# Transposing fp32 tiles as two 16-bit halves in 64-column tiles, in a fused four-layer graph-attention kernel

## The chip, the cores and the metric

One core of one Trainium2 chip. The metric is the device time of one execution in microseconds (us). All executions quoted here are of the fast state, with a mean granted TensorE clock of 0.995 to 0.997 in every profiled one. Engines: PE is TensorE, DVE is VectorE, ACT is ScalarE, POOL is GpSimd.

## The reference, cut to what matters

Sixteen graphs of 1024 nodes with 256 features, all fp32, one adjacency matrix. Four layers, each of this form:

```python
h = jnp.maximum(_layernorm(x, axis=-1), 0.0)
x = x + layer(h, adj, ...)          # four times

# layers 0 and 3 (four heads of 64 columns) and layer 1 (one head of 256):
q = h @ W
e = leaky_relu(s_src[:, None] + s_dst[None, :], 0.2)   # s = q . a, per node
e = where(adj > 0, e, -big)
out = elu(softmax(e) @ q)
# layer 2: e comes from (h W1)(h W2)^T, and the end is a relu
```

So each layer needs h transposed (features on partitions) for h @ W. These transposes are what the change is mostly about.

## The kernel before

All work is given to a small list scheduler inside the kernel (`plan.add(engine, cost, due, function, waits...)`): it simulates the engines with the costs given and emits the instructions in the resulting order. A cost there is a belief, not a measurement. `wide=True` marks PE work in 128-column shapes, between which and the rest the scheduler tries not to alternate.

Nearly all matrix products run in two column tiles of 64:

```python
def product(to, stationary, moving, start, stop):
    for c in range(0, P, COLS):                 # P = 128, COLS = 64
        nc.tensor.matmul(to[c : c + COLS], stationary[:, c : c + COLS], moving, ...)
```

The transposes of h did not; they are fp32 at the full 128 columns, two or four tiles of h at a time:

```python
run = 2 if direct else 4
...
tp = T["tp", t0] = buf("pp", [P, KC, 2 * P])                       # PSUM, fp32
for k in range(2):
    for c in range(KC):
        nc.tensor.transpose(tp[:, c, k * P : (k + 1) * P], T["h", t0 + k][:, c * P : (c + 1) * P], ident)
...
s = plan.add(PE, 0.44 * n, at, turned, norms, ..., wide=True)
...
nc.scalar.copy(T["hT", t0], T["tp", t0])                           # PSUM to SBUF, 512 words a partition
s = plan.add(ACT, 0.6, at, kept, (s,), ...)
...                                                                # then the projection, `product` with w[:, c, :cols]
cols = F + 3 * heads                                               # 268 columns with four heads, 259 with one
```

After the projection two exponentials per tile are taken of the extra columns and kept as factors; the factors of a layer are transposed too. The vectors `a` of layer 0 come with two transfers of short pieces. In the last layer each half of the nodes is closed (divide, ELU, add, store) for all four heads at once.

## Time and profile before

| of the kernel before | value | from |
|---|---|---|
| time | 3103.51 us (3102.70 to 3105.31, 4 runs) | the runs |
| PE / DVE / ACT busy | 99% / 88% / 44% | the page's first row |
| one steady period (one graph) | 188.3 us | starts of the same copy in neighbouring graphs |
| visits to 128-column shapes | 183 | instruction order |
| PE work, by its records | 2982 us | see below |
| time PE did no work: first 200 us / 200 to 2950 us / rest | 55.2 / 41.2 / 24.9 us | see below |

The last two rows will be used for every kernel. They are worked out, not read: each PE record of the profiled execution (for the kernel before one of 3104.86 us, 1.4 above its median) is counted at its own undisturbed spacing (29.17 ns for 65 columns, 108.75 for 257, 214.8 for 512, and so on, as the prediction lists them; a 16-bit transpose counts 56 ns at 128 columns or without a partner, and 27.9 ns in a pair of 64-column tiles), summed over a stretch, and taken from the stretch's length. A switch of shape counts as lost time in this account, which is good to a few tenths of a us. By the prediction's reading, the 41.2 us left in the middle stretch are the switches and nothing else: 149 of the visits lie there, 0.277 us each. That is why "PE 99% busy" is no reason to stop looking.

### The profile page before, as it was taken

The numbers are of one execution on the slowest core, as the hardware profiler recorded it, in microseconds if no ns is written. First come the engines' busy times: TensorE is split into PE (matmuls) and PEld (weight loads), VectorE is DVE, ScalarE is ACT, GpSimd is POOL, SyncE is SP. The second block draws the span as 40 slices with busy tenths as digits, with TensorE's granted clock in tenths as the row PEclk, the third lists the DMA queues.
The fourth block names the chain that finished last, engine by engine and source line by source line (L and its number), as shares of the span: only waits on it lengthen the run. The fifth ranks groups of instructions, "written<-read, shape, count | busy, mean of one in ns | idle before, by whom it ended". The sixth has DMA issues, their size and how long they took to land.

```text
span 3103.1 us, 108725 instructions
## 1 busy us (share of the span) xinstructions
PE 3058.2 (99%) x48836; PEld 2160.0 (70%) x48836; DVE 2716.4 (88%) x5532; ACT 1354.5 (44%) x3369; POOL 128.3 (4%) x99
## 2 busy tenths in 40 slices
PE   7899999999999999999999999999999999999998
PEld 5776757777676776767767676676767767665766
DVE  7999868999989899898989989899899989787797
ACT  5454465443533445334443433434334453345343
POOL 1000000000000000000000000000000000000000
PEclk9999999999999999999999999999999999999999
DMA  3111002102011110101102011020111101000110
GB/s 127 33 54 33 19 29 73 46 30 60 22 40 46 36 46 23 60 23 36 46 26 60 23 36 47 26 60 22 43 43 33 53 30 39 19 22 29 33 36 24
DMA packets 83577, 123.22 MB, mean 40 GB/s; under 512 B 8544, under 2 KB 44192, under 8 KB 83104
## 3 DMA queue, kind: packets, MB, share of 16 engines
q1 hardware_dynamic: 81776, 115.66, 12.4%
q8 instruction: 385, 6.31, 0.8%
q14 instruction: 88, 0.72, 0.1%
q10 hardware_dynamic: 1328, 0.52, 0.1%
HBM read 98.83 MB, written 17.33 MB: 37 GB/s over the span
## 4 chain that ended last, share of the span: by engine, by line
PE 96%; DVE 2%; DMA 1%; ACT 0%; issue 0%; POOL 0%; SPq 0%; POOLq 0%; DVEq 0%
PE pp L574 32%; PE acc L574 31%; PE accb L574 29%; PE pp L886 4%; DVE p L1063 1%; DMA a_bc<-in_L_gnn_a_dram 1%; DMA raw<-in_adj_dram 0%; DVE bn L800 0%; PE pp L998 0%; DVE xt L1041 0%; PE pp L982 0%; DVE o L1040 0%; DVE mv L801 0%; ACT junk_a L683 0%; POOL rstd L836 0%
## 5 line engine op out<-in xcount | busy, mean ns | idle before, releaser
L1063 DVE SCALAR_TENSOR_TENSOR p<-row,ke,mask 128x512 f32<-128x512 f32 x2048 | 1424.5, 745 | 94.5 <-PE acc L574 91.7
L574 PEld LDWEIGHTS acc<-val,p 128*64 128x64 f32 x32768 | 1066.9, 138 | 202.0 <-issue 109.0
L574 PE MATMUL acc<-val,p 128*64 128x65 f32 x32768 | 1095.4, 223 | 12.1 <-DVE p L1063 11.1
L574 PE MATMUL accb<-val,p 128*64 128x257 f32 x8192 | 926.1, 380 | 0.0
L574 PEld LDWEIGHTS accb<-val,p 128*64 128x64 f32 x8192 | 569.7, 136 | 291.3 <-issue 9.5
L574 PE MATMUL pp<-qT,hT 128*64 128x512 f32 x2048 | 471.5, 593 | 0.0
L574 PE MATMUL pp<-w,hTp 128*64 128x268 f32 (+1 forms) x3072 | 376.3, 388 | 0.7 <-ACT hTp L901 0.7
L1169 ACT ACTIVATE u<-pp 128x512 f32<-128x512 f32 x256 | 152.4, 595 | 323.2 <-PE pp L574 229.4
L574 PEld LDWEIGHTS pp<-w,hTp 128*64 128x64 f32 x3072 | 209.6, 137 | 107.8 <-issue 6.2
L870 ACT ACTIVATE h<-xt,nshift,rstd 128x256 f32<-128x256 f32 x512 | 272.5, 595 | 17.0 <-DVE nshift L839 15.7
L574 PEld LDWEIGHTS pp<-qT,hT 128*64 128x64 f32 x2048 | 133.0, 137 | 190.4 <-issue 184.9
L1209 ACT ACTIVATE o<-accb,rdens 128x256 f32<-128x256 f32 x128 | 60.7, 474 | 424.8 <-DVE rdens L1201 384.9
L800 DVE BATCH_NORM_STATS2 bn<-xt 128x6 f32<-128x256 f32 x512 | 212.5, 415 | 13.6 <-DMA xt<-in_x_dram 4.3
L836 POOL TENSOR_TENSOR rstd<-rstd,neg_half 128x8 f32<-128x8 f32 (+1 forms) x66 | 119.6, 1813 | 2371.9 <-DVE rstd L833 2094.5
L1207 ACT ACTIVATE o<-accb,rden 128x256 f32<-128x256 f32 x128 | 60.7, 475 | 336.4 <-DVE rden L1201 335.5
L1175 DVE TENSOR_TENSOR p<-p,mask 128x512 f32<-128x512 f32 x256 | 177.1, 692 | 8.9
L1142 DVE SCALAR_TENSOR_TENSOR p<-row,ke,mask 128x512 f32<-128x512 f32 x256 | 181.1, 743 | 0.0
L1174 DVE SCALAR_TENSOR_TENSOR p<-u,p 128x512 f32<-128x512 f32 x256 | 174.5, 682 | 5.9 <-ACT p L1170 5.7
L1170 ACT ACTIVATE p<-pp,shift_col 128x512 f32<-128x512 f32 x256 | 174.9, 683 | 0.0
L931 ACT ACTIVATE val<-pp 128x4 f32<-128x4 f32 (+1 forms) x384 | 66.8, 174 | 202.3 <-PE pp L574 202.2
L1040 DVE SCALAR_TENSOR_TENSOR o<-ex,o 128x256 f32<-128x256 f32 (+1 forms) x192 | 131.8, 686 | 16.0 <-ACT ex L1036 16.0
L901 ACT COPY hTp<-pp 128x512 f32<-128x512 f32 x192 | 104.6, 588 | 88.7 <-PE pp L886 88.6
(82 smaller groups left out, 1849.8 us busy)
## 6 DMA issues: line engine op xcount, KB each, us to landing
row<-er_d SPq DMA_DIRECT2D x272, 256.0 KB, 3.2
xt<-in_x_dram SPq DMA_DIRECT2D x32, 512.0 KB, 5.1
out_dram<-xt SPq DMA_DIRECT2D x32, 512.0 KB, 3.1
raw<-in_adj_dram SPq DMA_DIRECT2D x4, 1024.0 KB
raw<-in_adj_dram SPq DMA_DIRECT2D x16, 256.0 KB, 3.2
w<-in_L_gnn_W_dram SPq DMA_DIRECT2D x2, 256.0 KB
a_bc<-in_L_gnn_a_dram SPq DMA_DIRECT2D x4, 128.0 KB, 10.3
wraw<-in_L_gnn_W_dram SPq DMA_DIRECT2D x2, 256.0 KB
```

The source lines that it names most:

```text
L574: nc.tensor.matmul(to[c : c + COLS], stationary[:, c : c + COLS], moving, start=start, stop=stop, skip_group_check=True,)
L800: nc.vector.bn_stats(st, x_tiles[b][:, t, :])
L836: nc.gpsimd.tensor_tensor(T["rstd"][:, its], T["rstd"][:, its], neg_half[:, its], OP.pow)
L870: nc.scalar.activation(h, x_tiles[b][:, t, :], AF.Relu, bias=T["shift"][:, t : t + 1], scale=T["rstd"][:, t : t + 1],)
L886: nc.tensor.transpose(tp[:, c, k * P : (k + 1) * P], T["h", t0 + k][:, c * P : (c + 1) * P], ident)
L1040: nc.vector.scalar_tensor_tensor(o, ex, -1.0, o, op0=OP.mult, op1=OP.max)
L1063: nc.vector.scalar_tensor_tensor(p, lay.rows[half, hd], lay.ke[:, hd, jt : jt + 1], mask_of(half, jt), op0=OP.max, op1=OP.mult)
L1142: nc.vector.scalar_tensor_tensor(p, lay.rows[half, 0], lay.ke[:, 0, jt : jt + 1], mask_of(half, jt), op0=OP.max, op1=OP.mult)
L1169: nc.scalar.activation(u, e, AF.Exp, scale=1.0 - SLOPE)
L1170: nc.scalar.activation(p, e, AF.Exp, bias=shift_col, scale=SLOPE)
L1174: nc.vector.scalar_tensor_tensor(p, u, 1.0, p, op0=OP.max, op1=OP.mult)
L1175: nc.vector.tensor_mul(p, p, mask_of(half, jt))
```

## The change

Its intent: no switches in the steady part. An fp32 tile is read as pairs of 16-bit halves; each half is transposed as 16-bit data, bit for bit, in the two 64-column tiles that the products use; ACT puts the halves together when it copies from PSUM. Around that: one extra column per head less in the projection (one of the two exponentials is taken with a scale instead), vectors `a` in one transfer of 2 KB rows, the exponential's table loaded early, the first four tiles normalised ahead of the next four, and the last half of the last layer closed head by head. The scheduler's start times were fitted anew. The diff's core:

```diff
+    def turn(to, of):
+        n = of.shape[1]
+        for c in range(0, n, COLS):
+            nc.tensor.transpose(to[c : c + COLS], of[:, c : c + COLS], ident_b)
+    def halves(of):
+        return of.bitcast(BF16).rearrange("p (f s) -> p s f", s=2)
...
-                        tp = T["tp", t0] = buf("pp", [P, KC, 2 * P])
+                        tp = T["tp", t0] = buf("pp", [P, 2, KC, 2 * P], BF16)
                         for k in range(2):
+                            bits = halves(T["h", t0 + k])
                             for c in range(KC):
-                                nc.tensor.transpose(... T["h", t0 + k][:, c * P : (c + 1) * P], ident)
+                                for side in range(2):
+                                    turn(tp[:, side, c, k * P : (k + 1) * P], bits[:, side, c * P : (c + 1) * P])
-                s = plan.add(PE, 0.44 * n, at, turned, norms, ..., wide=True)
+                s = plan.add(PE, 0.47 * n, at, turned, norms, ...)
-                    nc.scalar.copy(T["hT", t0], T["tp", t0])
-                s = plan.add(ACT, 0.6, at, kept, (s,), ...)
+                    bits = T["hT", t0].bitcast(U16).rearrange("p c (q s) -> p s c q", s=2)
+                    nc.scalar.copy(bits, T["tp", t0].bitcast(U16))
+                s = plan.add(ACT, 0.95, at, kept, (s,), ...)
...
-            run = 2 if direct else 4
+            run = 2
-            cols = F + 3 * heads if self.gat else F
+            cols = F + 2 * heads if self.gat else F
...                                                 # `a` of a layer in one transfer:
+            queue.dma_start(
+                out=tiles["a"].rearrange("p h s d -> p (h s d)"),
+                in_=bass.AP(tensor=a.tensor, offset=a.offset, ap=[[0, P], [1, own * 2 * d]]),
+            )
...                                                 # front
+    plan.add(ACT, 1.6, SOON, warm)
+                at = due - 2 * (direct and n == 0)
-            stats = [statistics(b, t, due - 1, (loads[b][t],)) for t in range(NT)]
+            stats = [statistics(b, t, due - (3 if t < HT else 1), (loads[b][t],)) for t in range(NT)]
...                                                 # end
+            ending = lay.b == B - 1 and lay.layer == 3 and half == 1
+            if ending:
+                cols, sizes = (hd * d, (hd + 1) * d), (4, 0.8, 0.8)
```

The mask and factor transposes go through `turn` as well (cut here, like the new start times and the sign handling of `a`).

## The prediction

> **What bounds the kernel now.** I read the page first (busy shares, the 40 slices, the chain by line), then the groups by form, then the windows, and then the chain in order of time in one steady period, at the front and at the end.
>
> ```profile
> PE 3058.2 (99%) x48836; PEld 2160.0 (70%) x48836; DVE 2716.4 (88%) x5532; ACT 1354.5 (44%) x3369; POOL 128.3 (4%) x99
> ...
> PE   7899999999999999999999999999999999999998
> ...
> DVE  7999868999989899898989989899899989787797
> ...
> PE pp L574 32%; PE acc L574 31%; PE accb L574 29%; PE pp L886 4%; DVE p L1063 1%; DMA a_bc<-in_L_gnn_a_dram 1%; DMA raw<-in_adj_dram 0%; DVE bn L800 0%; PE pp L998 0%; DVE xt L1041 0%; PE pp L982 0%; DVE o L1040 0%; DVE mv L801 0%; ACT junk_a L683 0%; POOL rstd L836 0%
> ...
> L1063 DVE SCALAR_TENSOR_TENSOR p<-row,ke,mask 128x512 f32<-128x512 f32 x2048 | 1424.5, 745 | 94.5 <-PE acc L574 91.7
> ...
> L901 ACT COPY hTp<-pp 128x512 f32<-128x512 f32 x192 | 104.6, 588 | 88.7 <-PE pp L886 88.6
> ```
>
> The busy row and the slices say that PE works from the second slice to the last but one; the chain by line is 96% PE. DVE is second at 88%, ACT has room. But a busy PE is not a PE that does useful work: one steady stretch of the chain of waits shows what hides in it.
>
> ```profile
> 1025.79 0.47 PE acc L574 x16
> 1026.25 1.02 PE pp L886 x8
> 1027.28 1.08 PE acc L574 x32
> 1028.36 3.48 PE accb L574 x32
> ...
> 1049.29 0.93 PE acc L574 x32
> ```
>
> Thirty-two products take 0.93 us after other products and 1.08 us after eight transposes; and the eight transposes, 109 ns apart in the trace, take 1.02 us and not 0.87. So a visit to the 128-column transposes costs 0.30 us beyond its work. Starts in the trace say where: 152 instead of 52 ns from the last narrow product to the first transpose, 202 instead of 109 ns from the last transpose to the next product, and about 58 ns more between the first transposes. A second way: the chain repeats every 188.3 us (same pieces at 1086.58 and 1274.90). The records of one period at their own spacings (29.17 ns for 65 columns, 108.75 for 257, 214.8 for 512, 113.3 for 268, 109.6 for 259, 108.3 for 256, 109 per transpose) add up to 185.5 us. The missing 2.8 us over 10 visits are 0.277 us each. There is no other stall in the steady part.
>
> Front and end are limited by something else, DVE, since the four-head layers give it 0.66 us per weight tile (spacing in the trace) for 0.47 us of products:
>
> ```profile
> 13.08 0.42 DVE L666 TENSOR_TENSOR wa<-w,a_bc 128x256 f32<-128x256 f32 x1 [2.82 <-DMA a_bc<-in_L_gnn_a_dram]
> ...
> 17.29 1.28 ACT L870 ACT_TABLE_LOAD   x1 [17.29 <-DVE rstd L833]
> ...
> 21.33 5.11 PE L574 MATMUL pp<-w,hTp 128*64 128x268 f32 x32
> ...
> 29.24 2.74 DVE L1063 SCALAR_TENSOR_TENSOR p<-row,ke,mask 128x512 f32<-128x512 f32 x4 [0.30 <-ACT row L986]
> ...
> 38.10 0.76 DVE L940 TENSOR_TENSOR val<-pp,val 128x256 f32<-128x256 f32 x2 [2.67 <-ACT ke L932]
> ```
>
> ```profile
> 3092.53 0.20 DVE rden L1096
> ...
> 3092.75 0.94 ACT o L1107 x4
> ...
> 3093.71 1.06 ACT ex L1035
> ...
> 3094.79 1.06 ACT ex L1036
> ...
> 3095.88 1.24 DVE o L1040
> ...
> 3097.14 1.23 DVE xt L1041
> ```
>
> (The first fence is the timeline at the front, lines left out between; the second the chain at the end.) First weights at 29.24 us after waits for a small-packet load, a table load and the projections; at the end 5.8 us of closing behind the last products, then 4.7 us until the output is stored.
>
> **What the Trainium skill says.** "TensorEngine Tiling (Array Packing)", Key Properties: "Changing tiling mode (not just tile) drains the TensorE". The trace agrees and gives the price, 0.24 to 0.30 us per visit there and back; it is the shape and not the transposing, because a plain 128x128 product (L777) is also followed by 310 ns instead of 216. The same page, Feature Incompatibilities: column tiling excludes transpose mode for fp32 input. Hence the halves[...]. "TensorE: Matmul & The Clock Gate", section "Wait — 56ns, not 53.3ns?": N/2.4 GHz plus 2.5 ns, and starts never closer than about 25 ns. The 16-bit mask transposes here start 56 ns apart, as it says; the floor is not tested before. "ScalarE: Activation LUTs", What ACT_TABLE_LOAD costs: 0.833 ns per element, 1283 ns per load. The copies here (370 ns for 256, 588 for 512) give 0.85 ns, and the one load took 1283.
>
> **The change part by part.** The instruction order of both builds gives counts.
> 1. Visits to 128-column shapes fall from 183 to 18 (the row spreads of the first and last layers, weights, checks). 165 x 0.277 = -45.7 us.
> 2. 1024 fp32 transposes at 109 ns (111.6 us) become 4096 of 64 columns. The two column tiles alternate and should run side by side, as the product records do (starts about 10 ns apart in pairs); so a pair takes the 56 ns of a 16-bit transpose of 128 columns, 28 each, and I take 28.5: 116.7 us, +5.1.
> 3. 268 to 264 columns: 2048 records x 4/2.4 ns = -3.4; 259 to 258: 1024 x 0.42 ns = -0.4. The exponentials from one column less keep their number.
> 4. Factor transposes: 46 x 109 ns against 92 x 56 ns (one tile, no pairs): 0.
> PE work: -44.4 us. All of it at its old work plus switches is 3032.5 us, so 2988 us after.
> 5. ACT: 256 copies of 512 words become 1024 halves each. 588 + 512 x 0.85 ns = 1.02 us, +0.43, in all about +111 us on an engine with over 1700 us idle. Not on the path unless a projection waits for it.
> 6. Front. The vectors `a` come as one 2 KB row per partition, the table is loaded early, the first four tiles are normalised without waiting for the others. I add DVE rows to the second reduction of w0: ready near 17.3 us instead of 20.3. But the new order puts all eight projections ahead of the first row spread, so I expect the first weights near 28 us, not at 25, with 18.3 us of DVE work done instead of 14.5. DVE idle in the front falls by about 5 us there, and about 1 us more from the wait at 38.10. From about 26.4 to 20.5 us.
> 7. Behind it DVE stays the limit: DVE rows up to a weight tile plus all PE work from its products on exceed the PE total by at most 21.9 us before and 24.2 us after. PE gets cheaper, the DVE rows don't.
> 8. End. PE work to the last projection of the last layer, plus the DVE rows left, plus the ACT steps behind the last products: 17.6 us over the PE total before. After: the last quarter closes 256 columns instead of 1024 (2.7 instead of 5.8 us), but the earlier three quarters now stand between the weights on DVE (6 x 0.46 us), and more of the previous layer's weights stand behind that projection: 18.8 us.
> 9. Store: 4.7 to about 4.5.
>
> Before: 3032.5 + 21.9 + 17.6 + 26.4 + 4.7 = 3103.1 (the 26.4 is what was left; the DVE gaps in the trace up to 107 us, about 20, and rows slightly longer than my spacings make it up). After: 2988.2 + 24.2 + 18.8 + 20.5 + 4.5 = 3056 us, 1.5% less.
>
> **Rivals.**
> (a) Issue-bound transposes. Each needs an explicit weight load and a matmul, two instructions in 28 ns. Before, explicit pairs were 56 ns apart, and the products come two records to an instruction; nothing shows 14 ns per instruction. At 40 ns each the change loses 47 us and gains nothing: 3103. At 56 (no pairing) 3168. Against it: the schedule's own cost, 0.47 us for 16, is 29 ns, and its other costs match the trace.
> (b) A new drain between 16-bit and 32-bit products replaces the old one. At 0.1 us each way for some 170 visits, +34 us: 3090. Against it: one fp32 transpose followed by a 16-bit one in the trace took 109 ns, no more.
> (c) DVE becomes the bound in the steady part. It has 169 us of work per period, 90% of 188.3 and 91% of the new 185.6; order was refitted, but single waits may add 5 to 15 us: 3065.
> (d) Front and end gain more than I grant (rearranged on purpose): 10 to 15 us, 3042.
>
> **Range and chances.** The saving in the steady part is well measured, so the middle is narrow: 3045 to 3068 if (a) and (b) are false. I give (a) or (b) in part one chance in five, which stretches the upper side. 3040 to 3084 should hold 8 of 10. Faster by over 2% needs under 3041.5, so it needs (d) nearly whole: 0.15. Slower by 2% needs (a) in full: 0.02. Within 2%: 0.83.
>
> **What would show it.** A steady period near 185.6 us in the chain; 16 transposes in about 0.46 us; products after them at 0.93 us per 32. If the spacing is 40 ns or more, (a); if products after transposes still take longer, (b); gaps before products ended by DVE between 300 and 2800 us, (c). Copies near 1.0 us. First weights near 28 us, closing behind the last products near 2.7 us. The prediction is wrong in its middle if the front's DVE gaps do not shrink or shrink by over 10 us.

## The result, and the profile after

The changed kernel takes 3061.51 us (3061.14 to 3062.39, 4 runs) against 3103.51 us. The ratio is 0.9864, 95% interval 0.9847 to 0.9881: within 2%, a gain of 1.4%. (Ratios are the mean time of one kernel's fast runs over that of the other's fast runs of the same rounds, so not quite the ratio of the medians quoted.) Predicted: 3056, range 3040 to 3084.

From the page of the changed kernel: the busy row, the chain by line, and one group (busy us, mean ns of one, then idle time before):

```profile
PE 3017.0 (99%) x52018; PEld 2467.5 (81%) x52018; DVE 2722.5 (89%) x5551; ACT 1524.6 (50%) x3352; POOL 127.6 (4%) x115
...
PE pp L572 33%; PE accb L572 29%; PE acc L572 29%; PE pp L585 3%; DVE p L1089 3%; ACT hT L918 0%; ACT hTp L918 0%; DVE bn L813 0%; DVE xt L1066 0%; DMA xt<-in_x_dram 0%; DVE o L1065 0%; DVE mv L814 0%; PE pp L1002 0%; PE tpm L585 0%; PE er 
...
L918 ACT COPY hTp<-pp 128x1024 uint16<-128x1024 uint16 x192 | 248.8, 1324 | 54.9 <-PE pp L585 54.8
```

PE still bounds it, and the transposes (now line 585) fell from 4% of the chain to 3%. New in the chain is ACT, with line 918, which is the copy that puts the halves together: 1324 ns each where the old copy took 588 and the prediction said 1020. The chain of waits of the stretch from 1000 to 1120 us shows what it does:

```profile
1069.90 0.47 PE pp L585 x13
1070.37 0.02 issue
1070.40 1.36 ACT hT L918
1071.76 0.04 issue
1071.80 2.81 PE pp L572 x24
...
1079.21 0.89 PE pp L585 x32
1080.10 0.94 PE acc L572 x32
```

The last two lines are the change as intended: 32 transposes in 0.89 us, which is 28 ns each, then 32 products in 0.94 us, the undisturbed value; before, products after transposes took 1.08. These lines show no drain (the time that a switch of shape costs), neither the old one nor a new one between 16-bit and 32-bit data. But the lines above show PE waiting 1.4 us for a copy. In the whole stretch from 200 to 2950 us:

```profile
by line: PE pp L572 34.8%; PE accb L572 30.5%; PE acc L572 29.7%; PE pp L585 3.3%; ACT hT L918 0.5%; ACT hTp L918 0.3%; DVE p L1089 0.3%; issue 0.1%; PE er L585 0.1%; DVE parts L1308 0.1%; DVE bn L813 0.1%; DVE xt L1066 0.1%; DVE o L1065 0.
```

ACT copies hold 0.8% of 2750 us. In the kernel before the same row had no ACT entry:

```profile
by line: PE pp L574 34.2%; PE acc L574 30.7%; PE accb L574 30.4%; PE pp L886 4.3%; PE pp L998 0.3%; PE pp L1273 0.0%
```

The account by stretches:

| | PE work | idle 0 to 200 | idle 200 to 2950 | idle rest | steady period |
|---|---|---|---|---|---|
| before | 2982 us | 55.2 us | 41.2 us | 24.9 us | 188.3 us |
| after | 2981 us | 42.6 us | 10.8 us | 25.6 us | 186.3 us |

So the steady stretch gave 30 us, though the switches alone stood at 41; the front gave 13, PE work 1, and the end took 0.7. The period of 186.3 us misses the 185.6 that the prediction asked for.

At the front the chain in order of time shows the same copy, and the first weights (DVE line 1089):

```profile
25.22 1.32 ACT hTp L918
26.58 2.00 PE pp L572 x16
...
29.42 0.59 ACT row L1006
30.04 4.73 DVE p L1089 x7
```

The first weights come at 30.04 us. Before it was 29.24, and the prediction said 28. At the end, the steps behind the last products:

```profile
3052.60 0.19 DVE rden L1122
...
3054.63 0.42 DVE xt L1066
```

From 3052.60 to 3055.05 is 2.4 us of closing where it was 5.8; the store behind it takes until 3059.6, 4.5 us as predicted.

### The profile page after: what moved, and what is told of

Read it like the earlier page. It is cut to its first block, busy times and chain, and to the rows that moved or that the text cites. A ratio compares the mean times of both kernels' runs of the same rounds, so it can differ in the third digit from the quotient of the medians.

```text
span 3059.6 us, 115063 instructions
## 1 busy us (share of the span) xinstructions
PE 3017.0 (99%) x52018; PEld 2467.5 (81%) x52018; DVE 2722.5 (89%) x5551; ACT 1524.6 (50%) x3352; POOL 127.6 (4%) x115
## 4 chain that ended last, share of the span: by engine, by line
PE 94%; DVE 4%; ACT 1%; issue 0%; DMA 0%; SPq 0%; DVEq 0%; ACTq 0%
PE pp L572 33%; PE accb L572 29%; PE acc L572 29%; PE pp L585 3%; DVE p L1089 3%; ACT hT L918 0%; ACT hTp L918 0%; DVE bn L813 0%; DVE xt L1066 0%; DMA xt<-in_x_dram 0%; DVE o L1065 0%; DVE mv L814 0%; PE pp L1002 0%; PE tpm L585 0%; PE er L585 0%
## 5 line engine op out<-in xcount | busy, mean ns | idle before, releaser
L572 PE MATMUL acc<-val,p 128*64 128x65 f32 x32768 | 1080.9, 223 | 18.2 <-DVE p L1089 17.5
L572 PEld LDWEIGHTS accb<-val,p 128*64 128x64 f32 x8192 | 765.3, 137 | 103.6 <-issue 6.4
L572 PE MATMUL pp<-qT,hT 128*64 128x512 f32 x2048 | 457.7, 592 | 0.0
L572 PE MATMUL pp<-w,hTp 128*64 128x264 f32 (+1 forms) x3072 | 376.9, 386 | 1.3 <-ACT hTp L918 0.3
L572 PEld LDWEIGHTS pp<-qT,hT 128*64 128x64 f32 x2048 | 189.6, 137 | 205.9 <-issue 204.0
L572 PEld LDWEIGHTS pp<-w,hTp 128*64 128x64 f32 x3072 | 241.7, 137 | 81.0 <-ACT hTp L918 8.6
L918 ACT COPY hTp<-pp 128x1024 uint16<-128x1024 uint16 x192 | 248.8, 1324 | 54.9 <-PE pp L585 54.8
L1060 ACT ACTIVATE ex<-o 128x1024 f32<-128x1024 f32 (+1 forms) x195 | 122.1, 626 | 90.2 <-DVE o L1133 85.8
L585 PEld LDWEIGHTS <-h 128*64 128x64 bf16 x4096 | 145.5, 111 | 24.0 <-issue 13.3
```

Source lines behind the costliest of these rows:

```text
L585: nc.tensor.transpose(to[c : c + COLS], of[:, c : c + COLS], ident_b)
L918: nc.scalar.copy(bits, T["tp", t0].bitcast(U16))
L1060: nc.scalar.activation(ex, o, AF.Exp)
```

## The experiments

Two theories of why the steady stretch gave less than its switches. **A**: the halves themselves are fine, and the slow copy, later than the order of instructions assumes, makes PE wait. **B**: something of the halves on PE costs more than it seems (a remaining drain, the issue of twice the instructions), or the switches were worth less than read. Twelve kernels ran; all gave right results; the first one told below computes coarser numbers on purpose and still passed the comparison. The kernel before ran along in each batch; its medians were 3103.12, 3103.38, 3102.91 and 3102.80 us.

### The copy

**Only half of the data.** The changed kernel, but ACT copies the upper halves alone (512 elements, as 16-bit floats widened to fp32):

```diff
-                    bits = T["hT", t0].bitcast(U16).rearrange("p c (q s) -> p s c q", s=2)
-                    nc.scalar.copy(bits, T["tp", t0].bitcast(U16))
+                    nc.scalar.copy(T["hT", t0], T["tp", t0][:, 1])
```

> The changed kernel with ACT copying the upper halves alone, 512 elements instead of 1024 (numbers coarser on purpose, same transposes and order). Theory, the copy at 1.32 us instead of the 1.02 I had taken is what made the time 5 us longer than predicted: copy near 0.6 us, PE gaps ended by the copy gone, 3049 to 3055 us. Rival, the copies are hidden and DVE's front and end hold the rest: 3060 to 3062 us.

Measured: 3049.81 us (3047.89 to 3049.88, 4 runs), 11.7 us under the changed kernel. The copy took 587 ns, and the idle time in the steady stretch fell from 10.8 us to 0.0 in the account. PE ran exactly the same transposes. So theory B is out for the missing part: with the copy short, all of the 41 us of switches are gained.

**The same data, written side by side.** The same 1024 halves, but the two halves of a word are written one after the other; ACT now reads PSUM with a jump of 1 KB at every element instead of writing SBUF with a step of four bytes:

```diff
-                    bits = T["hT", t0].bitcast(U16).rearrange("p c (q s) -> p s c q", s=2)
-                    nc.scalar.copy(bits, T["tp", t0].bitcast(U16))
+                    bits = T["hT", t0].bitcast(U16).rearrange("p c (q s) -> p c q s", s=2)
+                    nc.scalar.copy(bits, T["tp", t0].bitcast(U16).rearrange("p s c q -> p c q s"))
```

> The changed kernel with the same 1024 halves copied in the other order: contiguous 16-bit writes, reads from PSUM that jump between the two sides. Right result. If the step of the write makes the copy slow (1.32 us against an estimate of 1.02): near 1.0 us and 3055 to 3058 us. If the 16-bit type or the count of elements does: 1.3 us and 3061 us. If the jumping read costs more: over 1.4 us and 3063 us or more.

Measured: 3049.79 us (3048.91 to 3050.82, 4 runs), ratio to before 0.9827 (0.9811 to 0.9844): right numbers, 1.7% under the kernel before and 11.7 us under the changed one; it beats both. The group row of the copy and the chain by line of the stretch from 200 to 2950 us:

```profile
L918 ACT COPY hTp<-pp 128x1024 uint16<-128x1024 uint16 x192 | 190.3, 1011 | 58.0 <-PE pp L585 56.7
```

```profile
by line: PE pp L572 34.5%; PE accb L572 30.6%; PE acc L572 30.5%; PE pp L585 3.6%; DVE p L1089 0.3%; PE er L585 0.1%; issue 0.1%; DVE parts L1308 0.1%; DVE bn L813 0.1%; DVE xt L1066 0.1%; DVE o L1065 0.1%; DVE parts L1307 0.0%; DVE mv L814
```

The copy takes 1011 ns, close to the predicted 1020, and ACT has left the chain. The account finds no idle time in the steady stretch (-0.2 us), and the period is 185.4 us, where the prediction said 185.6. The expected size was missed: the recorded expectation saw less to gain. It follows that neither the number of elements nor their type made the copy slow, but the step of the writes, or the order of elements that goes with it, which no run separates (the previous run read 16-bit data contiguously, too, at the usual rate). And a copy of 1.01 us costs no more than one of 0.59.

**The slow copy, and an order that knows of it.** The changed kernel with one number in its scheduler corrected; the copy itself stays at 1.3 us:

```diff
-                s = plan.add(ACT, 0.95, at, kept, (s,), ...)
+                s = plan.add(ACT, 1.3, at, kept, (s,), ...)
```

> The changed kernel with its slow copy (1.32 us) left as it is, but the kernel's own scheduler told 1.3 us for it instead of 0.95 us, so that it may place other products between a transpose and the projection that needs the copy; visits to 128-column shapes 20 instead of 18. Theory A (the 11.7 us were lost because the order was made for a copy of 0.95 us): most of it comes back, 3050 to 3054 us, and the share of ACT copies in the chain between 200 and 2950 us falls from 0.8% to under 0.3%. Theory B (the order has nothing to place there, or loses as much elsewhere, since its start times were fitted to the old cost): 3058 to 3066 us.

Measured: 3053.33 us (3052.31 to 3054.65, 4 runs), 8.2 of the 11.7 us back. From its page and from the same stretch of its chain:

```profile
L918 ACT COPY hTp<-pp 128x1024 uint16<-128x1024 uint16 x192 | 248.2, 1331 | 73.4 <-PE pp L585 73.3
```

```profile
by line: PE pp L572 34.6%; PE acc L572 30.9%; PE accb L572 30.5%; PE pp L585 3.5%; PE er L585 0.1%; DVE p L1089 0.1%; DVE bn L813 0.1%; issue 0.1%; DVE xt L1066 0.0%; DVE o L1065 0.0%; DVE mv L814 0.0%; ACT o L1244 0.0%; DVE o L1133 0.0%; P
```

The copy is as slow as ever (1331 ns) and yet gone from the chain; idle in the steady stretch is 2.0 us. So the loss was not the copy's length alone. It was a copy longer than the order was made for: the scheduler counted on the data 0.95 us behind the transposes, and in truth they came 1.3 us behind. (The number changes the order of the whole kernel, and 3.5 of the 11.7 us did not come back; what ties the gain to the copy is that ACT's copies left the chain.)

### The switches of shape

**Halves in full width.** The changed kernel with the 16-bit transposes at 128 columns: 239 visits instead of 18.

```diff
-        for c in range(0, n, COLS):
-            nc.tensor.transpose(to[c : c + COLS], of[:, c : c + COLS], ident_b)
+        nc.tensor.transpose(to[:n], of, ident_b)
```

> The changed kernel in the same order, its 16-bit halves transposed in 128-column tiles again, so 239 visits to 128-column shapes instead of 18. Theory, the drain comes with the shape: 221 x 0.277 us = 61 us more than the changed kernel, about 3122 us, and products after transposes slow again (1.08 us per 32). Rival, the price was that of fp32 transposes and 16-bit data takes it away: no change, about 3062 us. Transposing itself costs the same in both, 2048 x 56 ns.

Measured: 3106.6 us (3105.5 to 3107.47, 20 runs), slower than before by a ratio of 1.0011 (1.0004 to 1.0018) and 45 us over the changed kernel. The whole gain, and a little more, hangs on the narrow shape. No ACT copy appears in its chain between 200 and 2950 us although its copies are the slow ones. I took this to mean that the copies hide behind the switches, so that a visit costs (3106.6 - 3049.8) / 221 = 0.257 us. That needed a test.

**The same, with the side-by-side copy.**

> The fourth run's kernel with transposes in 128-column shapes, 239 visits to such shapes instead of 18 and 2048 transposes at 56 ns instead of 4096 at 27.6. Theory (a visit costs 0.257 us; in the first run the waits for copies hid behind the visits): 3049.8 + 221 x 0.257 = 3106.6 us, the same as the first run. Rival (the first run had both, 11.7 us of copy waits and the visits, so a visit costs (45.1 / 221) = 0.204 us): 3049.8 + 45.1 = 3094.9 us.

Measured: 3103.71 us (3102.34 to 3106.05, 12 runs). It lies between the two readings and nearer to the first: with 239 visits the slow copy costs 2.9 us where with 18 it costs 11.7. Against the side-by-side kernel with narrow transposes this is 53.9 us; 0.4 of them are the transposes themselves (2048 x 56 - 4096 x 27.9 ns, which the expectation left out; its 27.6 ns is a little low, since the pairs start 55 to 56 ns apart in the trace), so a visit costs 53.5 / 221 = 0.24 us. The chain shows one such visit:

```profile
1006.78 1.00 PE pp L584 x16
1007.78 1.08 PE acc L572 x32
```

Sixteen transposes at 56 ns are 0.90 us and take 1.00; the 32 products behind them take 1.08 instead of 0.93. Together 0.25 us.

**fp32 transposes in the changed kernel.** The changed kernel with h and factor tiles transposed and copied as before, but two tiles at a time as the new order has it: 286 visits.

```diff
-                            bits = halves(T["h", t0 + k])
                             for c in range(KC):
-                                for side in range(2):
-                                    turn(tp[:, side, c, k * P : (k + 1) * P], bits[:, side, c * P : (c + 1) * P])
+                                nc.tensor.transpose(
+                                    tp[:, c, k * P : (k + 1) * P], T["h", t0 + k][:, c * P : (c + 1) * P], ident
+                                )
...                                # fp32 copy, fp32 factors, wide=True and the old costs again
```

> The changed kernel with its h and factor tiles transposed in fp32 at full width again and copied as fp32 (0.59 us): 286 visits, because the new order transposes two tiles at a time where the old one took four. Theory (visits at 0.257 us are nearly all of it): 3049.8 + 268 x 0.257 = 3118.7, less 1.4 for the transposes: 3117 us, slower than before. Rival (a visit for fp32 costs what the prediction read, 0.277 us): 3049.8 + 74.2 - 1.4 = 3122.6 us. If the front, the closing and the columns alone made a good part of the gain, it would be under 3103 us.

Measured: 3123.0 us (3122.45 to 3123.6, 4 runs). Against the side-by-side kernel that is (3123.0 - 3049.8 + 2.7) / 268 = 0.283 us a visit (the 2.7 us are what the halves' transposes take more), near the 0.277 of the prediction; the rival named in the expectation holds. So an fp32 visit costs 0.28 and a 16-bit one 0.24. And front, closing and columns together do not make up for the 103 visits that this kernel has more than the one before.

**The halves alone, in the kernel before.** Only the transposes and the copy of h as halves, two tiles at a time; mask and factor transposes, front, closing and columns as before: 67 visits instead of 183. First with the slow copy, then with the side-by-side one.

```diff
-            run = 2 if direct else 4
+            run = 2
-                        tp = T["tp", t0] = buf("pp", [P, KC, 2 * P])
+                        tp = T["tp", t0] = buf("pp", [P, 2, KC, 2 * P], BF16)
...                                # turn() and halves() as in the change, cost 0.95 for the copy
```

> The kernel before with one part alone: its 1024 tile transposes as halves in 64-column tiles, with the copy of halves; old schedule constants, columns, front and closing. Visits 183 to 67. Theory: 116 x 0.277 = 32 us less, 2 us more for transposing, 5 to 10 us given back to slow copies: 3078 to 3084 us. Rival, front and closing made most of the gain: 3095 us or more.

Measured: 3094.64 us (3093.62 to 3095.13, 8 runs); missed by 10 us or more. The steady stretch lost only 14 of its 41 us of idle time, with the copies at 1327 ns and in the chain. The time is close to the rival's 3095 us, so this run alone did not decide; the next one does.

> The kernel before, with the h-tile transposes as halves and nothing else of the change, as in the second run, but with the copy that writes side by side (1.01 us) instead of with a step of four bytes (1.32 us). Theory (the copies alone took what was missing in the second run): 183 - 67 = 116 visits fewer at 0.257 us = -29.8 us, 4096 transposes at 27.6 ns against 1024 at 109 ns = +1.4 us, so 3103 - 28 = 3075 us, and no ACT copy in the chain between 200 and 2950 us. Rival (the old instruction order does not suit the halves, whatever the copy takes): 3088 to 3095 us as in the second run.

Measured: 3075.74 us (3075.21 to 3076.15, 4 runs), ratio 0.9911 (0.9896 to 0.9926), against 3075 expected. (That was worked out with 0.257 us a visit; with the 0.277 us of an fp32 visit and 27.9 ns a transpose it is 3074, which the interval holds as well.) The copies were all that was missing. Idle in the steady stretch is 11.3 us, about what the 44 visits left there cost. The front idles 53.0 us instead of 55.2; only 9 of the visits taken away lay in its 200 us, so these 2.2 us are about their price.

### Columns, closing, front

All four on the side-by-side kernel (3049.79 us), where no copy waits blur the difference.

**The columns put back** (268 and 259, the extra ones zero):

```diff
-                                pv[:, :cols],
+                                pv[:, :wide],          # wide = F + 3 * heads; w has zeros in the last `heads` columns
...
-                                w[:, c, :cols],
+                                w[:, c, :wide],
```

> The fourth run's kernel with the columns of the projections put back to 268 and 259 (the extra ones are zeros that nothing reads). Theory (step 3: PE time is columns at 2.4 per ns, and PE bounds these stretches): 2048 x 4/2.4 ns + 1024 x 0.42 ns = +3.8 us, 3053.6 us. Rival (the projections wait for copies or rows anyway in the four-head layers): under +1.5 us, below 3051.3 us.

Measured: 3053.61 us (3052.34 to 3054.74, 5 runs), +3.8 us, as worked out.

**The closing put back:**

```diff
-            ending = lay.b == B - 1 and lay.layer == 3 and half == 1
+            ending = False
```

> The fourth run's kernel (side-by-side copies) with the last half closed as before, all four heads in one pass at the end. Theory of the prediction's step 8 (the closing of the last quarter is shorter, but the three earlier quarters stand between the weights on DVE): closing 2.4 us becomes 5.8 us, +3.4, and 6 rows of 0.46 us leave the DVE queue ahead of it, -2.8: +0.6 us, 3050.4 us. Rival (those rows lie beside products and cost nothing): +3.4 us, 3053.2 us.

Measured: 3050.5 us (3049.48 to 3051.95, 5 runs), +0.7 us; the interval of one run overlaps the other's, so the direction rests on the traces too. The end of the chain, first with the new closing (the side-by-side kernel), then with the old:

```profile
3037.84 0.36 DVE o L1065
3038.22 0.42 DVE xt L1066
...
3041.42 0.19 DVE rden L1122
...
3043.45 0.42 DVE xt L1066
```

```profile
3038.85 0.19 DVE rden L1122
...
3040.03 1.06 ACT ex L1060
...
3043.46 1.23 DVE xt L1066
```

The old closing begins 2.6 us earlier (3038.85 instead of 3041.42), since the rows of the earlier quarters, like the two at 3037.84 and 3038.22, do not stand between the last weights on DVE; and it takes 3.4 us longer (5.8 us, to 3044.69, instead of 2.4). What is left is 0.8 us. A closing cut by more than half was worth under one microsecond.

**The front's order put back:** no early table load, statistics and first normalisation in the old places:

```diff
-    plan.add(ACT, 1.6, SOON, warm)
-                at = due - 2 * (direct and n == 0)
+                at = due
-            stats = [statistics(b, t, due - (3 if t < HT else 1), (loads[b][t],)) for t in range(NT)]
+            stats = [statistics(b, t, due - 1, (loads[b][t],)) for t in range(NT)]
```

> The fourth run's kernel with the front's three rearrangements undone: no early table load, no earlier place for the first statistics and the first four tiles' normalisation. The loads of the vectors a stay as changed. Theory (a DVE that waits in the front is lost time): first weights from 30.0 us to 32 to 33 us, the total +2 to +3 us, 3052 to 3053 us. Rival (the front is bound by the amount of DVE work, an order merely moves it): less than 1 us, under 3050.8 us.

Measured: 3050.99 us (3050.53 to 3052.35, 5 runs), +1.2 us, between the two expectations. Its timeline of PE has the first projection at 20.86 us; the side-by-side kernel's has it at 18.34. But the first weights, in the DVE timelines of this kernel and of the side-by-side one:

```profile
28.83 2.56 DVE L1088 SCALAR_TENSOR_TENSOR p<-row,ke,mask 128x512 f32<-128x512 f32 x3 [0.55 <-ACT row L1005]
```

```profile
30.18 4.72 DVE L1089 SCALAR_TENSOR_TENSOR p<-row,ke,mask 128x512 f32<-128x512 f32 x7
```

The slower kernel has its first weights 1.35 us earlier. So the moment of the first weights is no measure of this front. What DVE idles went with the time here: all its gaps up to 125 us add up to 16.3 us in the side-by-side kernel and 17.5 here, 1.2 us more, which is the difference in time. (They are 21.2 us in the kernel before and 16.1 in the changed one.) It is no sure measure either: in the kernel with the corrected cost the gaps are only 13.6 us, yet PE idles 43.0 us in the first 200 us, against 42.6 in the side-by-side kernel.

**The vectors `a` fetched as before,** in two transfers of short pieces; same instruction order:

```diff
-            queue.dma_start(
-                out=tiles["a"].rearrange("p h s d -> p (h s d)"),
-                in_=bass.AP(tensor=a.tensor, offset=a.offset, ap=[[0, P], [1, own * 2 * d]]),
-            )
+            for side in range(2):
+                queue.dma_start(
+                    out=tiles["a"][:, :, side, :],
+                    in_=bass.AP(tensor=a.tensor, offset=a.offset + side * d, ap=[[0, P], [2 * d, own], [1, d]]),
+                )
```

> The fourth run's kernel with the vectors a fetched as before, in two transfers of short pieces per layer instead of one of 2 KB rows; the instruction order is the same. Theory (what DVE idles in the front is lost time, as the seventh run showed: its DVE gaps up to 125 us grew from 16.3 to 17.5 us and the total grew by 1.2 us): the wait for a, 2.8 us in the kernel before, comes back in part, since the reductions now stand later: DVE gaps up by 1.5 to 3 us and the total by as much, 3051.3 to 3052.8 us. Rival (the transfer lands before DVE wants it in the new order): no change, 3049.8 us within 0.7.

Measured: 3051.61 us (3049.43 to 3052.66, 5 runs), +1.8 us in the medians and +1.2 in the means; its runs scatter, and the size is not settled better than that. The DVE timeline shows the wait itself, in brackets:

```profile
13.11 0.29 DVE L666 TENSOR_SCALAR a_bc<-a_bc 128x256 f32<-128x256 f32 x1 [2.59 <-DMA a_bc<-in_L_gnn_a_dram]
```

In the side-by-side kernel no wait stands before that row. The DVE gaps grow from 16.3 to 17.8 us, +1.5, in line with the time.

## Why the prediction was right or wrong

The total was right (3056 predicted, 3061.5 measured, inside the range), but the middle came so close partly by luck: the copy cost 11.7 us that the sum did not have, and cheaper transposes and a better front and end than granted made up for about 6 of them.

- **Bound, and step 1, the visits: right.** PE bounds the steady part, rivals (a) and (b) are out (28 ns a transpose, products behind them at 0.94 us per 32), and the price of 0.277 us per fp32 visit was found again as 0.283 in the run with 286 visits. The steady period without copy waits is 185.4 us, where 185.6 was worked out. Rival (c) would show as idle time in the steady stretch, and without the copy waits none is left there in the account.
- **Step 2, transposes: right in kind, too dear.** +5.1 us was predicted at 28.5 ns; the trace has 27.9 ns: 4096 x 27.9 - 1024 x 109 = +2.7 us. The term was mis-sized by 2.4 us.
- **Step 3, columns: right**, -3.8 us predicted and 3.8 measured.
- **Step 5, the copy: this is the step that failed.** "Not on the path unless a projection waits for it": projections did wait. The 1.02 us came from the number of elements; with a step of four bytes in the writes the same elements took 1.32 us, longer than the 0.95 us that the order was made for. That cost 11.7 us instead of 0. The prediction had the sign to look for on its list ("copies near 1.0 us"), but its rivals held no case of an ACT that is idle half the time and still late.
- **Step 6, the front: right by its own measure, not settled as a mechanism.** DVE idle was to fall by 5.9 us and its gaps fell by 5.1. But the first weights came at 30.04 us, not near 28, and the run with the old order showed that this time does not decide. PE's idle time in the first 200 us fell by 12.6 us: 16 of the visits taken away lay there, 4.4 us at 0.277 each; 1.2 us came with the order, 1.2 to 1.8 with the vectors. The rest, some 5 us, was not taken apart; that it comes from the new start times is a guess. To that extent rival (d) was in it.
- **Steps 7 to 9, the end: only the closing was tested, and it was right in size.** Undoing the new closing cost 0.7 us where step 8's reasoning, applied to the closing alone, gave 0.6. That there is a loss behind the gain (rows between the last weights) is shown by the two chains above. The 2.3 us that step 7 adds, and the previous layer's weights in step 8, no run checks.

The sum: 3056 - 2.4 + 11.7 = 3065.3, measured 3061.5. The remaining 3.8 us are in steps 6 to 9. Together these were to gain 2.6 us; outside the steady stretch, PE's idle time less 0.277 us for each visit there fell from 70.7 to 63.5 us, by 7.2. Which of the steps was mis-sized stays open with the 5 us above. The same remainder stands in the side-by-side kernel: 3056 - 2.4 = 3053.6, measured 3049.8.

## What to carry to other kernels

An engine at 50% can still be late: when an instruction on it gets longer, compare its new length with what the order of instructions assumes, and measure the length with the very access pattern, not by counting elements. Put the jumps of a re-ordering copy on the side where they are free (here the PSUM reads), and tell a scheduler the measured cost; either repair was worth 8 to 12 us on top of the change's 42. Where one engine bounds a stretch, count that engine's idle time; when some later stage first starts says little (here the kernel with first weights 1.35 us earlier was 1.2 us slower).

## What the Trainium skill lacked or had wrong

- "SBUF — State Buffer", section "Door 1: The DMA port swizzle", says that SBUF has 16-byte lines and that a step within them is free, up to eight 16-bit elements. The copy here stepped by two 16-bit elements when writing, well inside that, and took 1324 ns for 1024 elements instead of 1011. The same place gives PSUM 8-byte lines and says that jumps there slow matmuls; the copy that jumped 1 KB at each PSUM read paid nothing that shows (1011 ns, where 588 + 512 x 0.85 = 1023 was expected of a contiguous one). No page has a figure for either as ACT sees it.
- "ScalarE: Activation LUTs", section "What ACT_TABLE_LOAD costs", gives a fixed part and 0.833 ns per element for every function and both types, and nothing on the access pattern. That holds here (0.85 and 0.83 ns) for fp32 and for 16-bit data written side by side, not for the stepped write, which adds 0.31 ns per element.
- "TensorEngine Tiling (Array Packing)", Key Properties, says that changing the tiling mode drains TensorE, without a price. The runs give 0.28 us per visit there and back for fp32 transposes and 0.24 us for 16-bit ones.
- "TensorE: Matmul & The Clock Gate", section "Wait — 56ns, not 53.3ns?", names a floor of about 25 ns between starts, but no page has a figure for transposes in two column tiles: transposes with 128 moving columns that alternated between two 64-column tiles took 27.9 ns each (their pairs started 55 to 56 ns apart), half of the 56 ns of one tile. By the records the two of a pair mostly started under 10 ns apart, so that floor did not hold across two tiles.
